# A fused attention and convolution kernel: band weights turned in half pieces, weight maxima over memory, buffers moved, and the end of attention rearranged

## The chip, the cores and the metric

The kernel runs on one core of a Trainium2 chip. The metric is the device time of that core in microseconds: 3374.07 us before, the median of three runs (3363.94 to 3385.05). Five engines work side by side and meet at semaphores: TensorE (PE, with its weight loads as PEld), VectorE (DVE), ScalarE (ACT), GpSimd (POOL) and SyncE (SP, which issues nearly all DMAs).

## The reference, cut to what matters

The input x is (4, 128, 128, 128) in float32. Layer 0 cuts each image into overlapping 16x16 regions with a step of 14, normalises, attends inside each region with four heads, adds x, merges the overlaps, normalises again, projects to 256 channels, runs a depthwise 5x5 convolution, normalises over the batch, applies GELU twice and projects back. Layer 1 is two 3x3 convolutions with quantised activations and weights.

```python
attn = jax.nn.softmax(jnp.einsum('bhqd,bhkd->bhqk', q, k) * hd ** (-0.5), axis=-1)
o = jnp.einsum('bhqk,bhkd->bhqd', attn, v)
tok = o @ w_out + b_out + tok
...
ym = jax.lax.conv_general_dilated(ym, dw_k, window_strides=(1, 1), padding=[(2, 2), (2, 2)], feature_group_count=HIDDEN, ...)
...
alpha = jnp.max(jnp.abs(w)) + 1e-12
wc = jnp.clip(w / alpha, -1.0, 1.0)
q = jnp.round(wc * n) / n * alpha
```

## The kernel before

**Bands and regions.** Attention goes over 36 bands: four images, nine bands each, a band being sixteen rows. A band t has nine regions j. For each region the main loop (L834 to L850) issues `scores(j)`, then `last()`, which is the `values` step of the region before, then three lists of side work, with `halves(j)` and `values_in(j)` between them. The engines PE, ACT, DVE and SP execute in the order written here; only POOL's order is chosen by the scheduler. Every DMA that SP issues stands in one queue, so a DMA that has to wait holds all behind it.

**Side work.** `beside(t)` (L765) makes the nine triples of lists. The steps `a1`, `a2` are the first normalisation and the q and k projections of the next band's two row blocks (`ln1_chunks`); `b1`, `b2` are the output projection, the residual `xf`, the second normalisation and the projection `p0` to 256 channels of the last band's two row blocks (`post_chunks`). In both, a step of squares (ACT), one of sums on TensorE (L345), one of Ln and Exp on ACT that writes a small row of 1/deviation to memory (L362), one that reads it back spread over 128 partitions (`spread`, L367), and one that multiplies by it on DVE (`scaled`, L376). In `b1` and `b2` the multiply is step 6 and the four projections `p0` are steps 7 to 10.

**Conv steps.** The depthwise convolution is done on TensorE with band matrices, in units: one for each of the first three images (33 steps each), and three for the last image (17 steps each), whose rows come free only late. `conv_steps` (L545) gives a step that loads two tiles ahead, then one step a tile: load weights `w` (two DMAs) and rows `u` (four DMAs) for the tile after next, the products (L600), copies to `c` on ACT (L607), statistics on DVE (L611), and stores to `cv_d`. The list `todo` holds all steps that wait for a place; each band takes `share[0]` of them and sets each behind one region's side work: L792 names the order in which regions are filled.

```python
            conv = [todo.pop(0) for _ in range(min(share[0], len(todo)))]
...
            for j in sorted((0, 3, 5, 7, 1, 2, 8, 4, 6)[: len(conv)]):
                c[j] = [conv.pop(0)]
```

The unit over rows 64 to 95 of the last image enters `todo` at band 35 and gets nine places there; its last eight steps run in the tail.

**Preparation in the first bands.** `todo` begins with the quantisation of the two 3x3 weights (`quantised`, L281: load, largest, scales and clip, widen, to_int, to_f8) and with `band_matrices` (L202), which builds the depthwise band matrices over memory: zero edges, padded taps, 32 writes into `band_d`, then twelve pieces that are loaded, turned (outer two of three indices exchanged, L256) and stored to `dw_d`. Three places a band are used, so this takes bands 0 to 7. The turn of a piece is one copy of 40x2048, on ACT where the piece's s is odd and on DVE otherwise; one step turns two pieces and loads the next two. All these tiles share the three buffers of `scratch` (L198).

**Buffers.** `xp` (three) holds x row blocks `xt` that `load_ahead` (L409) loads from within the multiply step of the block in the same place one band earlier; `xfp` (one) holds `xf`, which is read until the multiply `b[6]`.

**The tail.** After the last region, `beside(T)` (L784) gives the `b` steps of the last band, with the eight conv steps that are left set between them, while POOL issues the sixteen loads of all conv weights `all_w` for the last unit (L861). Then the last unit runs with its own tiles: four loads ahead, products into the score tiles `sc`, stores by the ACT queue. After that follow the statistics and the gelu and 3x3 stages, which the change does not touch.

Of the kernel before, what the change touches and what calls it, by code (L numbers as in the profile page):

```python
# [14 lines left out]
P = 128  # L15
# [7 lines left out]
LB = 8  # L23
# [23 lines left out]
def layers(  # L47
# [127 lines left out]
    with ExitStack() as actx:  # L175
# [5 lines left out]
        work, dev, xnp, xfp = pool("work", 1), pool("dev", 2), pool("xnp", 3), pool("xfp", 1)  # L181
# [7 lines left out]
        xp, yp, sums = pool("xp", 3), pool("yp", 2), pool("sums", 1)  # L189
# [8 lines left out]
        def scratch(n):  # L198

            return up.tile([P, 32 * CW], F32, name="u")[:, :n]  # L200

        def band_matrices():  # L202
# [50 lines left out]
            def turn(c, s):  # L253
                by_c = scratch(32 * 64)[:KD]
                copy = nc.scalar.copy if s % 2 else nc.vector.tensor_copy
                copy(by_c.rearrange("p (c m) -> p m c", m=32), held.pop((c, s)))  # L256
                nc.sync.dma_start(
                    out=dw_d[c // 16 : (c + 64) // 16, :, s, :].rearrange("k p n -> p k n"),
                    in_=by_c.rearrange("p (k n) -> p k n", n=16 * 32),
                )  # L260

# [8 lines left out]
            steps = [several(zeros, *each(edges, [(b,) for b in range(B)])), padded_taps]  # L270
            for n in range(0, GR, 2):
                steps.append(several(*each(by_outputs, [(ro,) for ro in range(n, n + 2)])))
            steps += [lambda: None]

            for n in range(0, len(pieces) + 2, 2):
                steps.append(
                    several(*each(turn, pieces[max(n - 2, 0) : n]), *each(load, pieces[n : n + 2]))
                )
            return steps

        def quantised(n, w):  # L281
# [14 lines left out]
            def largest():  # L296
                am = small.tile([P, 1], F32, name="am")
                nc.vector.tensor_reduce(am, held["w"], AX.X, ALU.max, apply_absolute_value=True)
                held["alpha"] = small.tile([P, 1], F32, name="alpha")
                nc.gpsimd.partition_all_reduce(held["alpha"], am, P, bass_isa.ReduceOp.max)  # L300

            def scales():
                alpha = held["alpha"]
                nc.vector.tensor_scalar(alpha, alpha, 1e-12, None, ALU.add)
                nc.vector.tensor_scalar(ks, alpha, 1.0 / 105.0, None, ALU.mult)
                held["ra"] = small.tile([P, 1], F32, name="ra")
                nc.vector.reciprocal(held["ra"], alpha)
# [19 lines left out]
            return [load, largest, clip_all, widen, to_int, to_f8]  # L327
# [153 lines left out]
        def post_chunks(t):  # L481
# [4 lines left out]
            for at, (r, n) in enumerate(finished(t)):  # L486
# [5 lines left out]
                def project(hh, r=r, n=n, at=at, held=held):  # L492
                    if hh == 0:
                        room = tail[0] if tail and at else xfp
                        held["xf"] = room.tile([P, LB * P], F32, name="xf")
# [269 lines left out]
        def beside(t):  # L765
# [5 lines left out]
            if t >= 2:  # L771
                b, i = bands[t - 2]
                if i == NR - 1 and b < B - 1:
                    todo.extend(conv_steps(b))
                    share[0] = -(-len(todo) // (NR if b < B - 2 else 5))
                elif b == B - 1 and i == 4:
                    todo.extend(conv_steps(B - 1))
                    share[0] = NR
                elif b == B - 1 and i == 6:
                    todo.extend(conv_steps(B))  # L780
            conv = [todo.pop(0) for _ in range(min(share[0], len(todo)))]
            a1, a2 = one if one else ([None] * 9,) * 2
            b1, b2 = two if two else ([None] * 11,) * 2
            if t == T:  # L784
                c = conv + [None] * (9 - len(conv))
                return [
                    *b1[:2], *b2[:2], b1[2], b1[3], b2[2], b2[3], b1[4], b2[4], *c[:3], b1[5], b2[5],
                    *c[3:6], b1[6], *b1[7:], b2[6], *b2[7:], *c[6:],
                ]

            c = [[] for _ in range(NR)]
            for j in sorted((0, 3, 5, 7, 1, 2, 8, 4, 6)[: len(conv)]):  # L792
                c[j] = [conv.pop(0)]
            x1 = lambda: fetch(t, 0)
            x2 = lambda: fetch(t, 1)
            return [
# [4 lines left out]
                ([], [b1[6], a2[3], a1[5], a1[6], *c[4]], [b2[0], b2[1], b2[2]]),  # L801
                ([b2[3]], [a1[7], a1[8], *c[5]], [b2[4], a2[4], b1[7], b1[8]]),
                ([], [b2[5], b1[9], b1[10], *c[6]], [a2[5], a2[6]]),
                ([], [b2[6], x1, a2[7], a2[8]], c[7]),
                ([], [x2, b2[7], b2[8], *c[8]], [b2[9], b2[10]]),
            ]

# [8 lines left out]
        todo, share = [], [3]  # L816
        wq, kscale, tail = [], [], []
        for pair in zip(quantised(0, w1), quantised(1, w2)):
            todo.append(lambda pair=pair: [s() for s in pair])
# [9 lines left out]
        with nullcontext() if safe else tc.manual_schedule(engines=MANUAL):  # L829
# [27 lines left out]
            all_w = []  # L857
            for n, s in enumerate(beside(T)):
                if len(all_w) < NCK:
                    all_w.append(tail[0].tile([P, 3, 16, 32], F32, name=f"w{n}"))  # L860
                    weights(all_w[n], n, 0, 2, nc.gpsimd.dma_start)  # L861
                run([s])
            flush(len(stores))
            run(todo)
            for s in conv_steps(len(units) - 1, 4, (all_w, tail[1])):
                s()
                flush(len(stores), nc.scalar)

# [380 lines left out]
```

## Time and profile before

| what | value |
|---|---|
| median of three runs | 3374.07 us |
| profiled execution | 3383.11 us, of which the span is 3381.3 |
| mean granted TensorE clock | 0.960 |
| attention, first scores to last values | 35.4 to 2282.5 us |
| tail and last depthwise unit | 2282.5 to 2424 us |
| gelu and 3x3 stages | 2424 to 3381 us |
| memory traffic | 682.64 MB, 202 GB/s over the span |

The busy shares and the 40 slices say where TensorE is not at work; a window over one band gives its length and the busy time of each engine in it; the timeline then shows which instruction TensorE waited for there, and, from the instruction named, what that one had waited for. A wait for several semaphores is put down to the one that came last. A row of the timeline reads: start, length, engine, line, operation, written and read tiles, shape, count, and in brackets the idle time of the engine before it and what ended it.

The wait totals that the change bears on, over the whole run: POOL `sm` for ACT `pt` 629.7 us (125 times), PE L600 for loads of `u` 33.2 us (13), PE L446 for the DVE multiply 26.8 us (10), PE L345 for the residual `xf` 13.6 us (5), DVE multiply for the spread 60.2 us (22); on SP, waits for the rows of 1/deviation in front of L367, L386 and L569 231.8, 175.4 and 133.7 us.

### The profile page before, as it was taken

To read this page: it belongs to the slowest core of one execution; us is meant where nothing else is said; L and a number is where in the kernel's file an instruction comes from. 1 tells how busy PE (TensorE), PEld (TensorE's weight loads), DVE (VectorE), ACT (ScalarE), POOL (GpSimd) and SP (SyncE) were. 2 spreads that over 40 slices of the span, in tenths; PEclk is the share of its full clock that TensorE was granted. 3 is DMA by queue.
4 is the path that set the end of the run, shared out by engine and by line. 5 is a ranking of instruction groups with operands and counts; after the bars stand their busy time and mean duration, and the time that the engine had idled before them with its cause. 6 is when DMAs were issued, how large, how long until landed. Compare 5 with 4: busy or idle time off the path is not lost. (4 is left out here: it accounts for less than half of the span.)

```text
span 3381.3 us, 75962 instructions
## 1 busy us (share of the span) xinstructions
PE 3144.9 (93%) x30922; PEld 1584.0 (47%) x30922; DVE 2006.5 (59%) x3229; ACT 2006.7 (59%) x2818; POOL 841.9 (25%) x1060
## 2 busy tenths in 40 slices
PE   6999889999999999999999999984799999999998
PEld 3555445555454554554444445552544444444343
DVE  4767666766766666666655555551455555666543
ACT  4677667666666666666655556551267677433433
POOL 2443334333333333333322222220011111000000
PEclk8999989999999999999999999896599999999999
DMA  2455655788887788878699988877699999552298
GB/s 89 131 155 148 157 137 142 185 195 190 190 199 178 184 181 195 195 189 194 157 203 206 203 193 191 206 188 198 175 360 359 359 356 316 166 174 81 77 358 312
DMA packets 812012, 682.64 MB, mean 202 GB/s; under 512 B 581550, under 2 KB 696327, under 8 KB 811655
## 3 DMA queue, kind: packets, MB, share of 16 engines
q1 hardware_dynamic: 792071, 669.03, 72.8%
q10 hardware_dynamic: 18560, 4.72, 0.6%
q8 instruction: 247, 4.05, 0.5%
q0 software_dynamic: 1024, 3.93, 0.4%
q14 instruction: 110, 0.90, 0.1%
HBM read 410.68 MB, written 270.81 MB: 202 GB/s over the span
## 5 line engine op out<-in xcount | busy, mean ns | idle before, releaser
L751 DVE RECIPROCAL rd<-po 128x256 f32<-128x256 f32 x324 | 569.4, 1757 | 513.5 <-PE po L739 511.3
L1023 PE MATMUL pc<-q,wq 128*128 128x512 fp8e4 x3168 | 702.0, 381 | 14.4 <-DVE q L1035 14.4
L676 ACT ACTIVATE pt<-sc 128x1024 f32<-128x1024 f32 x648 | 626.2, 1019 | 96.5 <-PE sc L668 64.2
L686 POOL TENSOR_TENSOR sm<-pt 128x512 f32<-128x512 f32 x324 | 417.7, 1289 | 1064.3 <-ACT pt L676 629.7
L1023 PEld LDWEIGHTS <-wq 128*128 128x128 fp8e4 x3168 | 309.1, 98 | 417.6 <-issue 50.0
L600 PE MATMUL pm<-u,w 40*32 40x504 f32 (+5 forms) x7680 | 370.9, 497 | 48.3 <-DMA u<-y_d 33.2
L668 PE MATMUL sc<-q,kr 32*128 32x256 f32 x5184 | 402.4, 405 | 1.9 <-ACT pt L676 1.7
L731 PE MATMUL po<-pt,v 128*32 128x256 f32 x5184 | 349.9, 388 | 26.8 <-ACT v L660 16.7
L611 DVE BATCH_NORM_STATS2 st<-c 128x6 f32<-128x512 f32 (+2 forms) x384 | 175.4, 506 | 255.5 <-ACT c L607 254.7
L668 PEld LDWEIGHTS sc<-q,kr 32*128 32x128 f32 x5184 | 247.8, 185 | 150.3 <-issue 105.1
L607 ACT COPY c<-pm 128x512 f32<-128x512 f32 (+1 forms) x256 | 132.4, 562 | 288.9 <-PE pm L600 247.3
L446 PE MATMUL pm<-xn,wqkv 128*128 128x512 f32 (+1 forms) x576 | 270.2, 594 | 29.1 <-DVE xn L376 26.8
L515 PE MATMUL pm<-xn,wp 128*128 128x512 f32 (+1 forms) x576 | 259.7, 575 | 8.0 <-DVE xn L376 7.8
L656 PEld LDWEIGHTS pm<-wqkv,yr 128*128 128x128 f32 x1296 | 183.4, 194 | 177.5 <-issue 100.6
L600 PEld LDWEIGHTS pm<-u,w 40*32 40x32 f32 x7680 | 161.3, 110 | 218.4 <-issue 139.6
L1081 PE MATMUL pb<-cv,wp 128*128 128x512 f32 x512 | 232.6, 598 | 12.2 <-ACT cv L1072 12.2
L686 DVE TENSOR_TENSOR sm<-pt 128x512 f32<-128x512 f32 x324 | 228.2, 704 | 11.9 <-ACT pt L676 11.9
L520 ACT ACTIVATE y<-pm,bp 128x512 f32<-128x512 f32 (+1 forms) x288 | 180.5, 640 | 80.2 <-PE pm L515 73.8
L731 PEld LDWEIGHTS po<-pt,v 128*32 128x32 f32 x5184 | 137.1, 109 | 193.8 <-issue 47.8
L656 PE MATMUL pm<-wqkv,yr 128*128 128x128 f32 x1296 | 221.1, 294 | 1.8 <-DVE rstd L352 1.1
L739 PE MATMUL po<-sm,ones 128*32 128x256 f32 x2592 | 201.6, 381 | 8.0 <-POOL sm L686 8.0
L1031 DVE BATCH_NORM_STATS2 st<-pc 128x6 f32<-128x512 f32 x256 | 165.6, 689 | 67.3 <-PE pc L1023 67.3
(149 smaller groups left out, 3468.0 us busy)
## 6 DMA issues: line engine op xcount, KB each, us to landing
cv<-cv_d SPq DMA_DIRECT2D x64, 1024.0 KB
u<-y_d SPq DMA_DIRECT2D x224, 256.0 KB
cv_d<-c SPq DMA_DIRECT2D x192, 256.0 KB
xn<-row SPq DMA_DIRECT2D x80, 512.0 KB
y_d<-y SPq DMA_DIRECT2D x160, 256.0 KB
xfl<-xf_d SPq DMA_DIRECT2D x64, 512.0 KB
id_d<-y SPq DMA_DIRECT2D x64, 512.0 KB
idt<-id_d SPq DMA_DIRECT2D x64, 512.0 KB
```

The lines of the kernel that those rows point to most:

```text
L446: nc.tensor.matmul(pm[:, : n * P], wqkv[:, m * P : (m + 1) * P], held["xn"][hh], start=True, stop=True,)
L515: nc.tensor.matmul(pm[:, : n * P], wp0[:, h, :], held["xn"][hh], start=True, stop=True)
L600: nc.tensor.matmul(pc[half][32 * q : 32 * q + 32, j, :, a:z], wt[hs, s, c0 + c, :], ut[hs, :, c, a + s - 1 : z + s - 1], start=(s == 1), s ...
L656: nc.tensor.matmul(pv[:, c, :], region(yr, j)[:, c * P : (c + 1) * P], wqkv[:, 2 * P :], start=True, stop=True)
L668: nc.tensor.matmul(sc[h // 2][:, h % 2, kc, :].rearrange("p (r c) -> p r c", c=RS), region(kr, j)[hs, kc * P : (kc + 1) * P], queries(j, h ...
L676: nc.scalar.activation(pt, sc[p], AF.Exp)
L686: add(sm, pt[:, :, 0, :], pt[:, :, 1, :], ALU.add)
L731: nc.tensor.matmul(po[hs, 0, :], v[:, kc, hs], pt[h // 2][:, h % 2, kc, :], start=(kc == 0), stop=(kc == 1),)
L739: nc.tensor.matmul(po[hs, 1, :], ones, sm[h // 2][:, h % 2, :], start=True, stop=True)
L751: nc.vector.reciprocal(rd, po[:, 1, :])
L1023: nc.tensor.matmul(pc[:, h], w[:, t, :], q1[b][:, r + dy : r + dy + RB, dx : dx + P], start=(t == 0), stop=(t == 8),)
L1081: nc.tensor.matmul(pb[:, m], wp2[:, h, :], cv[:, h, px], start=(h == 0), stop=(h == 1))
```

## The change

- `xfp` gets two buffers, `xp` goes from three to two.
- `turn` copies half a piece at a time, always on DVE, in two steps; the next piece is loaded with the first half. Zeros, edges and band writes become single steps.
- The maximum over partitions is no longer a GpSimd all-reduce: the 128 partial maxima are written to memory as a row, read back into every partition as a 128x128 tile (`spread`), and reduced on DVE. The two weights' steps go one after the other, shifted by one, instead of in pairs.
- Seven places a band instead of three for this preparation, which then takes bands 0 to 8.
- The side plan is rearranged: `b1[6]` one region later, `b1[7..10]` and `a2[6]` after it.
- In band 35 the share is 18, two conv steps a region (`c[j]` and `d[j]`), so all 17 steps of that unit run there.
- The tail chain holds no conv steps; half of `all_w` is loaded by SP before it, the other half by SP after the first steps of the last unit. The second `xf` of the tail comes from `xfp`.

```diff
-        work, dev, xnp, xfp = pool("work", 1), pool("dev", 2), pool("xnp", 3), pool("xfp", 1)
+        work, dev, xnp, xfp = pool("work", 1), pool("dev", 2), pool("xnp", 3), pool("xfp", 2)
...
-        xp, yp, sums = pool("xp", 3), pool("yp", 2), pool("sums", 1)
+        xp, yp, sums = pool("xp", 2), pool("yp", 2), pool("sums", 1)
...
-            def turn(c, s):
-                by_c = scratch(32 * 64)[:KD]
-                copy = nc.scalar.copy if s % 2 else nc.vector.tensor_copy
-                copy(by_c.rearrange("p (c m) -> p m c", m=32), held.pop((c, s)))
-                nc.sync.dma_start(
...
+            def turn(c, s, half):
+                if half == 0:
+                    held["c"] = scratch(32 * 64)[:KD]
+                by_m, by_c = held[c, s], held["c"]
+                nc.vector.tensor_copy(
+                    by_c[:, half * 1024 : half * 1024 + 1024].rearrange("p (c m) -> p m c", m=32),
+                    by_m[:, :, 32 * half : 32 * half + 32],
+                )
+                if half:
+                    del held[c, s]
+                    nc.sync.dma_start(
...
-            for n in range(0, len(pieces) + 2, 2):
+            for n, p in enumerate(pieces):
                 steps.append(
-                    several(*each(turn, pieces[max(n - 2, 0) : n]), *each(load, pieces[n : n + 2]))
-                )
+                    several(lambda p=p: turn(*p, 0), *each(load, pieces[n + 1 : n + 2]))
+                )
+                steps.append(lambda p=p: turn(*p, 1))
...
-                held["alpha"] = small.tile([P, 1], F32, name="alpha")
-                nc.gpsimd.partition_all_reduce(held["alpha"], am, P, bass_isa.ReduceOp.max)
+                held["row"] = row = rowp.tile([4, 256], F32, name="row")
+                store(row[0:1, :P].rearrange("a p -> p a"), am)
+
+            def spread():
+                row = held["row"]
+                held["am"] = small.tile([P, P], F32, name="ams", bufs=1)
+                nc.sync.dma_start(out=held["am"], in_=bass.AP(row.tensor, row.offset, [[0, P], [1, P]]))
...
+                nc.vector.tensor_reduce(alpha, held["am"], AX.X, ALU.max)
...
                 elif b == B - 1 and i == 6:
                     todo.extend(conv_steps(B))
+                    share[0] = 2 * NR
...
-                    *b1[:2], *b2[:2], b1[2], b1[3], b2[2], b2[3], b1[4], b2[4], *c[:3], b1[5], b2[5],
-                    *c[3:6], b1[6], *b1[7:], b2[6], *b2[7:], *c[6:],
+                    *conv, *b1[:2], *b2[:2], b1[2], b1[3], b2[2], b2[3], b1[4], b2[4], b1[5], b2[5],
+                    b1[6], *b1[7:], b2[6], *b2[7:],
...
-                ([], [b1[6], a2[3], a1[5], a1[6], *c[4]], [b2[0], b2[1], b2[2]]),
-                ([b2[3]], [a1[7], a1[8], *c[5]], [b2[4], a2[4], b1[7], b1[8]]),
-                ([], [b2[5], b1[9], b1[10], *c[6]], [a2[5], a2[6]]),
-                ([], [b2[6], x1, a2[7], a2[8]], c[7]),
+                ([], [a2[3], a1[5], a1[6], *c[4]], [b2[0], b2[1], b2[2]]),
+                ([b2[3]], [b1[6], a1[7], a1[8], *c[5]], [b2[4], a2[4]]),
+                ([], [b2[5], b1[7], b1[8], *c[6]], [b1[9], b1[10], a2[5]]),
+                ([], [b2[6], x1, a2[6], a2[7], a2[8]], c[7]),
                 ([], [x2, b2[7], b2[8], *c[8]], [b2[9], b2[10]]),
             ]
+            return [(one, two, three + d[j]) for j, (one, two, three) in enumerate(plan)]
...
-        todo, share = [], [3]
+        todo, share = [], [7]
...
-            all_w = []
-            for n, s in enumerate(beside(T)):
-                if len(all_w) < NCK:
-                    all_w.append(tail[0].tile([P, 3, 16, 32], F32, name=f"w{n}"))
-                    weights(all_w[n], n, 0, 2, nc.gpsimd.dma_start)
-                run([s])
+            all_w = [tail[0].tile([P, 3, 16, 32], F32, name=f"w{k}") for k in range(NCK)]
+            for k in range(NCK // 2):
+                weights(all_w[k], k, 0, 2, nc.sync.dma_start)
+            run(beside(T))
             flush(len(stores))
             run(todo)
-            for s in conv_steps(len(units) - 1, 4, (all_w, tail[1])):
+            for n, s in enumerate(conv_steps(len(units) - 1, 4, (all_w, tail[1]))):
                 s()
                 flush(len(stores), nc.scalar)
+                if n < NCK // 2:
+                    weights(all_w[NCK // 2 + n], NCK // 2 + n, 0, 2, nc.sync.dma_start)
```

## The prediction

> **What bounds the kernel now.** I read the page first (busy shares, 40 slices), then windows over each band of nine regions (from the first scores matmul, L668, of one band to that of the next), then the timeline wherever TensorE's idle time rose.
>
> ```profile
> PE 3144.9 (93%) x30922; PEld 1584.0 (47%) x30922; DVE 2006.5 (59%) x3229; ACT 2006.7 (59%) x2818; POOL 841.9 (25%) x1060
> ...
> PE   6999889999999999999999999984799999999998
> ...
> PEclk8999989999999999999999999896599999999999
> ```
>
> TensorE is the bound almost everywhere; the dents are in slices 0, 4-5 and around 30.
>
> ```profile
> 297.40:348.70 51.30, 49.41 (x505) 26.88 (x504) 36.06 (x55) 37.12 (x60) 21.65 (x28) 1.00 0.57 149
> 348.70:417.80 69.10, 53.78 (x501) 28.77 (x500) 42.34 (x59) 44.49 (x62) 24.33 (x27) 0.90 0.62 152
> 417.80:485.40 67.60, 54.49 (x502) 29.02 (x502) 42.37 (x59) 44.31 (x61) 23.19 (x24) 0.87 0.57 146
> ...
> 1188.20:1249.00 60.80, 59.70 (x693) 30.50 (x692) 40.80 (x63) 41.16 (x68) 20.98 (x27) 1.00 0.80 190
> 1669.50:1746.20 76.70, 68.82 (x789) 32.73 (x788) 42.97 (x67) 43.95 (x71) 19.48 (x25) 0.96 0.93 188
> ...
> 2216.20:2282.50 66.30, 58.77 (x1245) 35.18 (x1244) 37.88 (x79) 35.32 (x61) 19.09 (x23) 0.95 0.69 177
> 2282.50:2366.00 83.50, 38.95 (x824) 23.54 (x825) 16.45 (x48) 15.65 (x32) 8.33 (x17) 0.64 0.78 198
> 2366.00:2424.00 58.00, 46.06 (x1536) 39.80 (x1536) 25.07 (x125) 10.35 (x32) 0.00 (x0) 0.50 0.63 155
> ```
>
> Columns: stretch, length, busy us of PE, PEld, DVE, ACT, POOL, clock, DMA share, GB/s. A plain band takes 51.3 us; bands 6 and 7, equal in attention work, take 69.1 and 67.6. A band with four conv steps is nearly all matmul (59.7 of 60.8). With seven (bands 28 to 32), TensorE idles 4 to 8 us. From 2282.5, when attention ends, TensorE idles 44.5 of 83.5 us, then works at half clock. After 2424 nothing is changed; the chain of waits is TensorE alone from 2470 on (L1023, L1081), and before that, back to 2254 where it breaks off, it is mostly loads of `u` and stores of `cv_d`: the tail hangs on transfers, the rest on TensorE.
>
> ```profile
> 59.24 0.72 POOL L300 PARTITION_ALL_REDUCE alpha<-am  x2 [5.77 <-issue]
> 60.91 1.07 PE L731 MATMUL po<-pt,v 128*32 128x256 f32 x16
> 69.95 1.08 PE L739 MATMUL po<-sm,ones 128*32 128x256 f32 x8 [7.97 <-POOL sm L686]
> ...
> 354.14 1.95 DVE L256 COPY u<-u 40x2048 f32<-40x2048 f32 x1
> 356.13 3.67 ACT L256 COPY u<-u 40x2048 f32<-40x2048 f32 x1 [3.33 <-DVE u L256]
> 360.07 1.94 PE L731 MATMUL po<-pt,v 128*32 128x256 f32 x16 [7.03 <-ACT v L660]
> ...
> 1710.69 1.29 DVE L376 TENSOR_TENSOR xn<-xn,xf 128x512 f32<-128x512 f32 x2 [5.04 <-DMA xn<-row]
> 1712.76 1.38 PE L345 MATMUL pm<-xf,ones 128*32 128x192 f32 x8 [4.32 <-DVE xf L500]
> ...
> 2307.65 0.48 ACTq L362 DMA_DIRECT2D row<-rstd  x1
> ```
>
> Four causes, one each: the two all-reduces keep POOL from its `sm` (8.0 us); two whole turns, one after the other, keep ACT from `v` (7.0 us, in both bands); the residual's multiply waits for its spread on DVE and the next residual stands behind it (4.3 us); in the tail the first row of rstd, ready at 2298, is issued at 2307.65.
>
> **What the Trainium skill says.** "TensorE: Matmul & The Clock Gate" (What's actually happening) gives half clock after an idle window of about 3.4 us: agreed, 0.64 and 0.50 above, and four L446 matmuls after the all-reduce took 3.78 us where the same four at 57 us took 1.98. "DMA: Bandwidth & Descriptors" (Issuing engines are not separate DMA queues) says that another issuer only saves issue time, so moving weight loads from POOL to SP moves 0.39 us each, no bytes; no run here compares the two. Its section Latency and other measured facts names a fixed cost of about 2 us per DMA, hence an estimate of 4 us for two in a row; here a row written at 16.42 was back, spread over 512 KB, at 21.87: 5.5 us, which I use.
>
> **The change part by part**, against the profiled execution, 3383.1 us (span 3381.3), 9.0 above the median 3374.07.
>
> *Maxima over memory.* POOL loses two all-reduces; added are two 128-element writes, two 64 KB reads on SP and two 128x128 maxima on DVE (about 0.28 us, as L163 of that size). The wait for a trip of 5.5 us or less lies between two conv slots (regions of 5.7 us); what SP holds behind it is x and residual loads wanted a band later. Gone: 8.0 us and about 2 us of cold matmuls. DVE may wait a little for the read, with `rd` behind it. **-9** (-5 to -11).
>
> *Half turns.* Excess of bands 6 and 7: 69.1 + 67.6 - 2 x 51.3 = 34.1 us. In its place 24 half copies, all on DVE, about 1.0 us each (half of 1.95), over bands 5 to 8; the built order shows one a region, behind that region's `sm`. Cover: DVE is busy 36 of 51.3 us in a plain band, so 1.7 us a region is free and `rd` usually waits for PE. I charge 0.2 us each, 5 us: **-29**. Bounds: all 24 exposed, -10; none, -34. Splitting zeros, edges and band writes into single steps moves the same DMAs to other regions of bands whose DMA share is 0.6: nothing, +-2.
>
> *Residual buffer and later multiply.* `b1[6]` moves a region later, so `b2[0]` no longer stands behind a late spread; it needs the second `xf`. In 1669 to 2046 PE waited 12.7 us for `xf`, and a clock of 0.96 over 377 us lost about as much again. Next in line is DMA at 0.93, so I take a third: **-9** (0 to -20). The projections that move (`a2[6]`, `b1[7..10]`) keep their number; where bands are all matmul, 0 (-3 to +6).
>
> *x buffers.* Pool `xp` goes from three to two, so each x load now waits on SP for the DVE multiply of two blocks earlier; behind it stand stores, spreads and conv loads. Comparing, block by block, the end of that multiply with the issue of the load in this trace: in 21 of 70 cases the multiply is later (84 us together, 19 at most), nearly all in bands without conv work; elsewhere it was over by about 4 us. 0, up to +6.
>
> *Last band.* Seventeen steps instead of nine: eight more products at 1.71 us (13.70 us for 8 in this window) are 13.7 us of PE. DMA per step, from the trace's packets: 240 of 1 KB, 160 of 2 KB, 1024 of 256 B at 57, 112 and 19 ns over 16 engines, 3.2 us, eight are 26 on top of 0.69 x 66.3 = 46: 72 us. SP issues some 168 DMAs in the built order at 0.39 us, 66 us. All three come close to each other, so the band becomes about 83 us: **+17** (+13 to +30).
>
> *Tail chain.* From end of attention to the first `sc` matmul of the last unit it is 83.5 us. Without conv, from the rows of before: last values and seams 4.3 (2288.3 less 1.5 of POOL's DMA issues), projection to rstd 9.6, Ln and Exp 0.9, trip 5.5, first multiply 0.7, p0 and y 12.4 (2344.5 to 2356.9; the second spread hides in it), landing 3.5, load 5: 42 us. Four of eight weight pairs now go on SP ahead: 8 issues are 3.1 us, 1.97 MB at about 200 GB/s 10 us, partly in front of the rows: +6. So **-35** (-25 to -41). The last unit stays as it is: half clock, 55 us; the other four weight pairs add 7 us to DMA at 0.63 of 58.
>
> Sum: -9 - 29 - 9 + 17 - 35 = **-65**: 3318 by the profiled execution, **3309** by the median.
>
> **Rivals.**
> - *The end gives it back*: band 35 becomes bound by SP and DMA (+30) and the rows wait behind the weights (-25): +5 in place of -18. For: 168 issues and DMA at 72 us in one band. Against: bands of 88 us run at DMA 0.88 with little idle. 3332.
> - *DVE becomes the bound in bands 5 to 8*: each half turn exposed, and waits for its load: -10 there, 3328.
> - *The x loads hold SP*: slower. A multiply not yet done blocks SP and so the conv loads behind it. At 72 loads, 0.9 us of PE each eats the whole gain; at 1.5 us, 108 - 65 = +43, 3417. It decides only if SP arrives before the multiply in conv bands; the trace has it 4 us late, and PE waited for `u` 33 us in the whole run.
> - *It does not do what it says*: the words say more buffers of x, the diff gives fewer; the half turns could have been put together. The built order shows them apart, so I give it nothing of its own.
>
> **How the numbers follow.** Forecast 0.62 (own range 3280 to 3335), end gives back 0.20, DVE 0.11, x loads 0.07. The first three reach, with their bounds, from 3280 to 3358; outside are the x loads and about a tenth of the rest. About 1%, 34 us, is what a measurement of this kernel can tell from no change: faster if below 3340. Nearly all of the forecast, six in ten of the second and seven in ten of the third fall there: 0.60 + 0.12 + 0.08, less a little: 0.79. Slower is the x loads, 0.07; within 1% 0.14.
>
> **What would show it.** Right: no idle of 7 us on PE up to 500 us; bands 5 to 8 of 51 to 54 us; no `xf` wait over 2 us in bands 28 to 32; band 35 of 80 to 86 us; 45 to 50 us from the end of attention to the first `sc`. Wrong: bands 10 to 27 over 61.5 us, SP waiting for DVE at the x loads there; band 35 over 95 us; rows still issued late behind weights.

## The result, and the profile after

The changed kernel takes 3343.9 us (median of seven runs, 3342.32 to 3353.07) where the kernel before, run beside it, takes 3380.13 (3363.94 to 3385.05). The ratio is 0.9908, 95% interval 0.9887 to 0.9929: faster, by 36 us in the medians and 31 by the ratio, where 65 were forecast. The profiled executions, 3348.1 and 3383.11 us, differ by 35.

In the changed kernel lines stand 10 to 12 lower in attention: scores L679, values L742 and L750, multiply L388, spread L379, row L374, stores L398, turn L257, `w` and `u` loads L551 and L580, conv products L611, copy `c` L618. The page of the profile after, the same rows as before (busy time, then tenths in 40 slices):

```profile
PE 3129.4 (94%) x30922; PEld 1594.7 (48%) x30922; DVE 2008.2 (60%) x3247; ACT 1998.7 (60%) x2814; POOL 815.9 (24%) x1042
...
PE   7996999999999999999999989875699999999998
...
PEclk9998999999999999999999998976599999999999
```

PEclk is full in slice 0 now, but slice 3, which was full, has a dent, and the dents around slice 30 begin earlier. Windows of the profile after, band by band and then the end (columns as before: stretch, length, busy PE, PEld, DVE, ACT, POOL, clock, DMA share, GB/s):

```profile
226.70:294.00 67.30, 51.70 (x501) 28.46 (x500) 35.00 (x55) 37.61 (x60) 20.50 (x28) 0.87 0.43 125
294.00:360.30 66.30, 50.46 (x505) 27.69 (x504) 37.16 (x58) 37.60 (x60) 21.93 (x28) 0.90 0.45 121
360.30:411.20 50.90, 48.53 (x501) 27.07 (x500) 41.68 (x63) 37.38 (x60) 22.27 (x27) 1.00 0.64 171
...
1215.40:1275.20 59.80, 59.23 (x693) 30.69 (x692) 40.59 (x63) 41.50 (x68) 20.26 (x27) 1.00 0.83 199
...
2166.10:2282.70 116.60, 87.92 (x2013) 56.20 (x2012) 45.34 (x111) 41.18 (x77) 17.19 (x20) 0.77 0.65 169
2282.70:2319.30 36.60, 16.78 (x64) 6.79 (x62) 9.34 (x16) 10.00 (x16) 1.78 (x4) 0.79 0.68 192
2319.30:2388.10 68.80, 49.34 (x1536) 39.81 (x1536) 23.42 (x116) 9.70 (x30) 0.00 (x0) 0.50 0.60 156
```

The first two are bands 4 and 5: 67 and 66 us of plain attention that took 51.3 before, at the lowest DMA share of all. The third is band 6; bands 6 and 7, 69.1 and 67.6 before, take 51. The fourth has four conv steps. The last three are band 35, the tail and the last conv unit. All stages of the two profiles, with what the prediction said of each:

| stage | before | after | difference | forecast |
|---|---|---|---|---|
| band 0 | 52.5 | 40.2 | -12.3 | -9 |
| bands 1 to 3 | 158.2 | 152.0 | -6.2 | 0 |
| bands 4 and 5 | 102.6 | 133.6 | +31.0 | 0, but for its part of the 5 us charged for half turns |
| bands 6 to 8 | 188.4 | 154.4 | -34.0 | -29 with band 5 |
| bands 10 to 27 | 1080.6 | 1063.4 | -17.2 | 0 |
| bands 28 to 32 | 376.2 | 360.9 | -15.3 | -9 |
| bands 33 and 34 | 170.6 | 175.4 | +4.8 | 0 |
| band 35 | 66.3 | 116.6 | +50.3 | +17 |
| end of attention to first `sc` | 83.5 | 36.5 | -47.0 | -35 |
| last conv unit | 55.1 | 68.8 | +13.7 | 0 |

What follows takes 960.2 and 958.1 us, the start 1.0 less; band 9 is alike. Bands 4 and 5, band 35 and the last unit lost 95 us that the sum had at 17; the stages that gained brought 132 us that it had at 82. That the total missed by no more than 30 us is luck: errors of 78 and 50 us went opposite ways.

### The profile page after: what moved, and what is told of

The parts are those of the page before. It is cut to its first block, busy times and chain, and to the rows that moved or that the text cites. A ratio compares the mean times of both kernels' runs of the same rounds, so it can differ in the third digit from the quotient of the medians.

```text
span 3346.2 us, 76089 instructions
## 1 busy us (share of the span) xinstructions
PE 3129.4 (94%) x30922; PEld 1594.7 (48%) x30922; DVE 2008.2 (60%) x3247; ACT 1998.7 (60%) x2814; POOL 815.9 (24%) x1042
## 4 chain that ended last, share of the span: by engine, by line
PE 73%; DMA 9%; ACT 7%; DVE 5%; SPq 2%; issue 2%; ACTq 1%; POOL 0%; DVEq 0%; POOLq 0%
PE pc L1040 19%; PE pm L611 9%; PE sc L679 7%; PE pm L458 7%; PE po L742 7%; PE pb L1098 6%; PE pm L526 6%; PE pm L667 4%; PE pm L510 3%; PE po L750 3%; DMA u<-y_d 3%; DMA xn<-row 2%; ACT pt L687 2%; PE pm L357 2%; DMA cv_d<-c 2%
## 5 line engine op out<-in xcount | busy, mean ns | idle before, releaser
L611 PE MATMUL pm<-u,w 40*32 40x504 f32 (+5 forms) x7680 | 378.3, 500 | 42.0 <-DMA u<-y_d 33.7
L679 PE MATMUL sc<-q,kr 32*128 32x256 f32 x5184 | 407.3, 409 | 1.9 <-ACT pt L687 1.7
L742 PE MATMUL po<-pt,v 128*32 128x256 f32 x5184 | 352.2, 390 | 11.7 <-DVE part L766 11.6
L679 PEld LDWEIGHTS sc<-q,kr 32*128 32x128 f32 x5184 | 250.5, 187 | 129.6 <-issue 80.2
L458 PE MATMUL pm<-xn,wqkv 128*128 128x512 f32 (+1 forms) x576 | 262.9, 581 | 50.7 <-DVE xn L388 50.7
L618 ACT COPY c<-pm 128x512 f32<-128x512 f32 (+1 forms) x256 | 132.8, 562 | 295.2 <-PE pm L611 263.8
L611 PEld LDWEIGHTS pm<-u,w 40*32 40x32 f32 x7680 | 167.0, 111 | 208.6 <-issue 119.4
L742 PEld LDWEIGHTS po<-pt,v 128*32 128x32 f32 x5184 | 137.8, 110 | 180.0 <-issue 50.4
L750 PE MATMUL po<-sm,ones 128*32 128x256 f32 x2592 | 201.8, 382 | 0.0
```

The lines of the kernel that those rows point to most:

```text
L458: nc.tensor.matmul(pm[:, : n * P], wqkv[:, m * P : (m + 1) * P], held["xn"][hh], start=True, stop=True,)
L611: nc.tensor.matmul(pc[half][32 * q : 32 * q + 32, j, :, a:z], wt[hs, s, c0 + c, :], ut[hs, :, c, a + s - 1 : z + s - 1], start=(s == 1), s ...
L679: nc.tensor.matmul(sc[h // 2][:, h % 2, kc, :].rearrange("p (r c) -> p r c", c=RS), region(kr, j)[hs, kc * P : (kc + 1) * P], queries(j, h ...
L742: nc.tensor.matmul(po[hs, 0, :], v[:, kc, hs], pt[h // 2][:, h % 2, kc, :], start=(kc == 0), stop=(kc == 1),)
L750: nc.tensor.matmul(po[hs, 1, :], ones, sm[h // 2][:, h % 2, :], start=True, stop=True)
```

## The stall in bands 4 and 5

From the timeline of the profile after, in band 4 (start, length, engine, line, what is written and read, count, in brackets the idle time before and what ended it):

```profile
238.03 0.50 ACTq L374 DMA_DIRECT2D row<-rstd  x1
239.69 5.86 SPq L398 DMA_DIRECT2D y_d<-y  x3
243.54 0.48 ACTq L374 DMA_DIRECT2D row<-rstd  x1
...
248.56 0.48 ACTq L374 DMA_DIRECT2D row<-rstd  x1
...
250.16 2.82 SPq L237 DMA_DIRECT2D band_d<-pad_d  x4
253.09 0.40 SPq L398 DMA_DIRECT2D xf_d<-xf  x1
253.59 0.37 SPq L379 DMA_DIRECT2D xn<-row  x1
...
262.87 1.29 DVE L388 TENSOR_TENSOR xn<-xn,xt 128x512 f32<-128x512 f32 x2 [14.62 <-DMA xn<-row]
...
263.61 3.78 PE L458 MATMUL pm<-xn,wqkv 128*128 128x512 f32 x4 [14.25 <-DVE xn L388]
```

Read it upwards. TensorE waits 14.25 us for the multiply, the multiply for the spread. The row that this spread reads was issued by ACT at 238.03; SP issues the spread only at 253.59. In between SP stores `y_d` and writes `band_d`, and each time starts 1.6 us after another row of ACT: 239.69 after 238.03, 250.16 after 248.56 (the third `y_d` store, at 245.19, after 243.54). None of them reads a row. The DMAs of SP and ACT signal their end on eight semaphores, numbered 101 to 107 and 109 in the trace, which the two engines take in turn: these are the completion counters in the texts below. A DMA waits here until the one before it on its counter has ended. The row of 238.03 and the first `y_d` store share counter 107, the row of 243.54 and the third store 101, the row of 248.56 and the first `band_d` write 102. So SP waits for the third row before it may issue the spread of the first.

That explains the late issue. From its issue to the multiply the spread took 9.3 us more, against 3.8 for the first spread of the kernel before (18.10 to 21.87), while the four writes issued just before it were still in transfer. How much of the 9.3 us is theirs is not shown.

**Pairs again.** First theory: the single writes stand in front of the spread.

```diff
-            steps += each(by_outputs, [(ro,) for ro in range(GR)])
+            for n in (0, 4):
+                steps += [two(n), idle, idle, two(n + 1), two(n + 2), two(n + 3), idle]
```

> The changed kernel, with the writes to band_d in pairs again, in regions 0, 3, 5 and 7 of bands 3 and 4; nothing else differs. Theory (single writes in regions 0 to 2 stand on SP, and on the DMA rings, in front of the spread xn of ln1, which then reaches DVE late): the stalls of 14.3 and 14.5 us at L458 in bands 4 and 5 go, both bands take 51 to 54 us in place of 67.3 and 66.3, and the whole takes 24 to 30 us less than the changed kernel, about 3316. Rival (two buffers of x, not the writes, hold the first multiply): both bands stay at 66 to 67 us and the time at 3344.

Ratio 0.9906 (0.9887 to 0.9925), where the changed kernel has 0.9908. Bands 4 and 5 took 65.7 and 60.5 us, TensorE's waits there 13.8 and 7.5 us, again for the multiply. That theory fell, and its rival, x buffers, was not shown either.

**Writes by POOL.**

```diff
-                    nc.sync.dma_start(
+                    nc.gpsimd.dma_start(
                         out=band_d[2 * ro + eo]
```

> The changed kernel, with the 32 writes to band_d issued by POOL in place of SP, in the same places. Theory (on SP they stand in front of the ln1 spread, and they wait there for rows of rstd that ACT writes only later; the bytes themselves do no harm): SP no longer waits for a row before the spread, the spread is issued within 2 us of its row, bands 4 and 5 take 51 to 54 us each in place of 67.3 and 66.3, the whole 24 to 31 us less than the changed kernel, about 3316. Rival (the writes fill the DMA rings and the spread lands late behind them, whoever issues it): the spread goes out early but DVE still waits 8 us or more for it, bands 4 and 5 stay above 60 us each, the whole is at most 10 us less.

Ratio 0.9839 (0.9822 to 0.9856). Bands 4 and 5: 53.8 and 53.1 us. The bytes are the same and TensorE waits for no multiply in the two bands, so the bytes alone are not the cause. But this edit takes the writes out of SP's order and off the counters together.

**Rows by POOL.** The writes stay on SP, in front of the spread; only the rows leave ACT.

```diff
-                nc.scalar.dma_start(out=row[:, :w], in_=rstd[0:P:32, :])
+                by = nc.gpsimd if 3 <= now[0] <= 5 else nc.scalar
+                by.dma_start(out=row[:, :w], in_=rstd[0:P:32, :])
```

> The changed kernel, with the rows of rstd of bands 3 to 5 issued by POOL in place of ACT; the writes to band_d stay on SP, in their places. Theory (SP's stores and writes wait there for a row that ACT issues later, because the DMAs of SP and ACT take the same few completion counters in turn; the order on SP is harmless otherwise): without ACT's rows on these counters SP reaches the spread of ln1 when its row has landed, and bands 4 and 5 take 51 to 57 us each in place of 67.3 and 66.3, the whole 18 to 30 us less than the changed kernel. Rival (it is the order on SP: the spread stands behind four writes, whatever they wait for): bands 4 and 5 stay at 62 to 68 us each, the whole within 8 us of the changed kernel.

Ratio 0.9827 (0.9810 to 0.9845), bands 4 and 5 49.1 us each, below a plain band of either kernel. The same place in this kernel's timeline:

```profile
226.95 3.29 SPq L399 DMA_DIRECT2D y_d<-y  x3
230.29 4.28 SPq L237 DMA_DIRECT2D band_d<-pad_d  x4
238.20 0.34 SPq L399 DMA_DIRECT2D xf_d<-xf  x1
238.25 0.62 POOL L375 DMA_DIRECT2D row<-rstd  x1 [2.95 <-ACT rstd L372]
242.40 0.34 SPq L380 DMA_DIRECT2D xn<-row  x1
...
247.21 1.28 DVE L389 TENSOR_TENSOR xn<-xn,xt 128x512 f32<-128x512 f32 x2
```

Stores and writes are out before the first row exists, the spread follows its row by 4 us, and DVE has no idle time in front of the multiply. With the same order on SP the stall is gone, so the wait for rows was the cause. The 35.4 us of the two bands are far more than ACT saves by not issuing their eight rows, 0.48 us each.

## Band 35

Two conv steps in the timeline of SP, profile after, and below them what SP's DMAs of the band cost to issue (count; ns minimum, median, maximum; first and last start), asked by line:

```profile
2204.95 1.56 SPq L551 DMA_DIRECT2D w<-dw_d  x2
2206.56 1.57 SPq L580 DMA_DIRECT2D u<-y_d  x4
2208.23 1.94 SPq L398 DMA_DIRECT2D cv_d<-c  x4
2210.27 1.57 SPq L551 DMA_DIRECT2D w<-dw_d  x2
2211.88 1.57 SPq L580 DMA_DIRECT2D u<-y_d  x4
```

```profile
L551 SPq DMA_DIRECT2D w<-dw_d x32: 747/760/789, 2172.4 to 2269.5; - x32
```

```profile
L580 SPq DMA_DIRECT2D u<-y_d x64: 296/324/1536, 2174.1 to 2271.6; - x64
```

```profile
L398 SPq DMA_DIRECT2D cv_d<-c x68: 360/467/1489, 2167.9 to 2281.6; - x68
```

One step is 5.1 us of SP without a gap; two a region make 10.2 us, where a plain region takes 5.7. Weights, `u` and conv stores are 24.4, 26.3 and 35.0 us in all, and SP's issuing in the band, 181 DMAs, is 94. That is what the Trainium skill, in "Perfetto Trace Analysis" (What "DMA-bound" means), lists as its second case: the issuing engine's track is solid with DMA slices, which are time spent making descriptors, not moving data. The trace agrees in part: DMA share 0.65, SP at 94 of 116.6 us.

**Nine steps again**, the tail's order with it:

```diff
-                    share[0] = 2 * NR
...
+                    *b1[:2], *b2[:2], b1[2], b1[3], b2[2], b2[3], b1[4], b2[4], *c[:3], b1[5], b2[5],
+                    *c[3:6], b1[6], *b1[7:], b2[6], *b2[7:], *c[6:],
```

> The changed kernel, with nine conv steps in the last band again, and the other eight between the steps of the tail chain as before. Theory (the last band lost 50 us, more than the tail gained): band 35 takes 66 to 70 us in place of about 116, the stretch from end of attention to the end of the last conv unit about 138 in place of 106, and the whole 14 to 20 us less than the changed kernel: about 3327. Rival (most of the 50 us in band 35 is something else than the eight added steps, such as loads that come late after the change of buffers): band 35 stays above 90 us and the whole is 10 us or more above the changed kernel.

Band 35: 63.4 us, so the 50 us are the eight steps. But from there to the last conv product it took 153.7 us, not 138, since the last unit stayed at 68.7; ratio 0.9906 (0.9886 to 0.9926), the same as with the change.

**Weights by POOL:** `nc.gpsimd.dma_start` for the `w` loads of this unit.

> The changed kernel, with the two weight loads of each conv step of the last band issued by POOL in place of SP. Theory (SP's issuing bounds band 35: 5.1 us a step, two steps a region): SP loses 1.57 us a step, so a region falls from 10.2 to about 7.1 us and then to the next bound, TensorE and DMA at 71 to 75 us a band: band 35 takes 78 to 92 us in place of about 116, the whole 24 to 38 us less than the changed kernel, about 3313. Rival (three buffers of weights and u, two steps ahead, are too few, or the DMA rings themselves are): the issue moves and the landing does not, band 35 stays at 108 to 118 us and the whole at 3338 to 3346.

Band 35: 104.0 us, 12.6 less for 24 us less of weights to issue; between theory and rival. Ratio 0.9893 (0.9873 to 0.9912). In five kernels that are alike in this band it took 111.9 to 118.0 us, so single profiles of it differ by some 6 us.

**Conv stores by ACT as well.**

> The kernel that has POOL issue the weight loads of the last band, with the conv stores of that band issued by ACT as well, so that SP is left with 35 us of issuing of the 94 us that it has in the changed kernel. Theory (what is left of band 35 is still SP's issuing): up to the end of attention it takes 82 to 92 us in place of 104 with POOL's weights and 116.6 in the changed kernel, the whole 10 to 20 us less than with POOL's weights alone. Rival (with 75 us of issuing in 104 SP had ceased to be the bound; loads two steps ahead in three buffers, and TensorE at a lowered clock, are): 98 to 108 us, and the whole within 6 us of the one with POOL's weights.

Band 35: 96.4 us, between the two; ratio 0.9887 (0.9868 to 0.9906). SP's waits in that band say why the rest did not follow:

```profile
SPq L580 <- DMA cv_d<-c: 24.1, 9, 5.5
```

The loads of `u` now waited 24.1 us, nine times, for stores that ACT issues: the counters again.

**Conv stores by POOL**, weights on SP.

> The changed kernel, with the conv stores of the last band issued by POOL in place of SP (weights stay on SP). With ACT as their issuer SP's u loads waited 24.1 us for these stores. Theory (band 35 is SP's issuing, 94 us, and what remained with ACT as issuer was SP waiting for ACT's DMAs through the shared counters): SP is left with 60 us, u loads no longer wait for stores, band 35 takes 84 to 93 us up to the end of attention in place of 116.6, and of 96.4 with weights by POOL and stores by ACT. Rival (loads only two steps ahead, or TensorE at a lowered clock, bound it at 95 to 105 whoever issues): 95 or more.

100.2 us, ratio 0.9855 (0.9829 to 0.9882). Waits of `u` for stores are gone, yet TensorE still waited 15.4 us for `u`, 7.3 of it for the first load, which is issued in the region of its product; and SP's weight loads still waited 8.3 us for rows. So 12 to 20 us of the 50 went with SP's issuing, give or take that spread. A floor of 95 to 105 us (the kernels below among them) remains. Loads only two steps ahead and a clock of 0.84 to 0.87 are candidates; a deeper lookahead was not tried, so that floor stays open.

## The last unit

TensorE's waits there, from the first `sc` matmul on, in the profile after (in all, times, longest), then in the kernel below:

```profile
PE sc L611 <- DMA u<-y_d: 19.8, 11, 6.9
PE sc L611 <- DMA w<-dw_d: 3.7, 1, 3.7
```

```profile
PE sc L611 <- DMA u<-y_d: 7.4, 2, 7.1
PE sc L611 <- issue: 4.0, 6, 0.9
```

**All weights in the tail**, by POOL, as before:

```diff
-            for k in range(NCK // 2):
-                weights(all_w[k], k, 0, 2, nc.sync.dma_start)
-            run(beside(T))
+            for n, s in enumerate(beside(T)):
+                if len(all_w) < NCK:
+                    all_w.append(tail[0].tile([P, 3, 16, 32], F32, name=f"w{n}"))
+                    weights(all_w[n], n, 0, 2, nc.gpsimd.dma_start)
+                run([s])
```

> The changed kernel, with all eight weight pairs of the last conv unit loaded by POOL between the steps of the tail chain, as before, and none within the unit. Theory (the 13.7 us by which the last unit got longer come from four weight pairs that SP issues between its u loads): from the first sc matmul to the last 55 to 58 us in place of 68.8; from the end of attention to the first sc 36 to 44 us in place of 36.5, as more bytes go in front; the whole 7 to 14 us less than the changed kernel, about 3333. Rival (the unit is slower because its u loads are not as far ahead as they were behind other conv work): it stays at 66 to 70 us, the whole at 3343 to 3352.

The unit took 55.0 us, the stretch before it 42.9: 13.8 gained, 6.4 given back. Ratio 0.9891 (0.9875 to 0.9907), an interval too wide to show these 7 us.

SP's own waits in the last unit of the changed kernel, most of them in its first steps, say how the weights did it:

```profile
SPq L580 <- DMA cv_d<-c: 17.0, 8, 7.6
SPq L551 <- DMA cv_d<-c: 5.0, 3, 3.9
```

SP waited 22.0 us for conv stores that ACT issues here and that neither load reads: the counters again. Issuing the eight weight loads took 2.3 us in all. Without weights in the unit there is no such wait: a step then has four `u` loads and four stores, and the eight counters keep apart, 101 and 104 to 106 for the loads, 102, 103, 107 and 109 for the stores. Each pair of weights shifts the turn by two, and loads fall on the counters of stores.

## The order of the steps

**Order and residual buffer as before** (one `xf`, the tail's second from its own pool), then the **order alone**, with two `xf`:

```diff
-                ([], [a2[3], a1[5], a1[6], *c[4]], [b2[0], b2[1], b2[2]]),
-                ([b2[3]], [b1[6], a1[7], a1[8], *c[5]], [b2[4], a2[4]]),
...
+                ([], [b1[6], a2[3], a1[5], a1[6], *c[4]], [b2[0], b2[1], b2[2]]),
+                ([b2[3]], [a1[7], a1[8], *c[5]], [b2[4], a2[4], b1[7], b1[8]]),
```

> The changed kernel, with the order of the steps in a band and the one buffer of the residual as before (the multiply b1[6] back in region 4, a2[6] and the b1 projections a region earlier). Theory (this part freed bands 28 to 32 of 15 us, and also made the bands with four conv steps 1.1 us shorter each): bands 28 to 32 take 372 to 378 us in all in place of 361, bands 10 to 26 about 60.9 each in place of 59.8, the whole 26 to 36 us more than the changed kernel, about 3374. Rival (the 1.1 us of each conv band come from the two buffers of x or from chance): only bands 28 to 32 lose, 9 to 16 us, and the whole is about 3355.

> The changed kernel, with the order of the steps in a band as before, and the second buffer of the residual kept. Theory (the order alone, with the first multiply of the second norm and the projections a region later, made each band with four conv steps 1.1 us shorter): bands 10 to 27 take 1078 to 1082 us in all as before, in place of 1063.4, the whole 20 to 36 us more than the changed kernel, as with order and buffer both undone (3386 us, 1080.4). Rival (the second residual buffer did it): bands 10 to 27 stay at 1062 to 1066 us, the whole at 3343 to 3355.

Ratios 1.0010 (1.0000 to 1.0021) and 0.9993 (0.9984 to 1.0003); bands 10 to 27 took 1080.4 and 1079.5 us, bands 28 to 32 371.2 and 370.1, bands 1 to 3 157.5 and 156.1, bands 6 to 8 157.8 and 157.3. So the order alone took some 16 us out of the bands that the prediction held for all matmul: idle time per conv band fell from 1.1 to 0.6 us, and PE's busy time by half a microsecond. Over the whole run, undoing the order alone costs 0.0085 of the time before, about 29 us, nearly all that the change gains. TensorE's waits in bands 10 to 27, before and after, are almost all for ACT's squares:

```profile
PE pm L345 <- ACT sq L339: 16.1, 34, 0.7
```

```profile
PE pm L357 <- ACT sq L351: 10.6, 19, 0.7
```

Why PE's busy time fell too is not shown. Bands 10 to 27 of the second kernel have two x buffers and the length of the kernel before, which has three: x loads cost nothing there. Of bands 28 to 32 nothing so exact can be said: in eleven kernels that are alike there they took 360.9 (the changed kernel itself) to 375.9 us, mean 368.2, and the two with the order as before lie within that range.

## The repairs together

**Three repairs** (writes, all weights of the last unit and band 35's weights by POOL, its conv stores by ACT), and **nine steps with the first two**:

> The changed kernel with three repairs together: the writes to band_d by POOL, all weights of the last unit by POOL within the tail chain, and in the last band the weights by POOL and the conv stores by ACT. Theory (the three places don't touch each other): 27 + 8 + 20 us less than the changed kernel, about 3290; bands 4 and 5 of 51 to 54 us, band 35 of 92 to 100, the last unit of 55 to 58. Rival (what one repair gains, the next stage waits for, as in bands 28 to 34, whose length differs by 10 us between kernels that are alike there): 3305 or more.

> The kernel that has nine conv steps in the last band and eight in the tail chain, with the writes to band_d by POOL and all weights of the last unit by POOL within the tail. Theory (two steps a region pay once SP is relieved of a part of its issuing): band 35 takes 63 to 66 us, end of attention to last conv product 136 to 144, together 199 to 210 where the kernel with all three repairs has 190 to 200: 5 to 15 us more than that kernel. Rival (two steps a region gain nothing even then): the two are within 4 us.

Ratios 0.9803 (0.9777 to 0.9828) and 0.9812 (0.9791 to 0.9833). The three repairs gained 36 us on the changed kernel, of 55 expected; band 35 took 104.6 us, where the same two edits had given 96.4. Band 35 up to the last conv product: 205.5 and 203.8 us. Two steps a region were worth nothing here.

**All rows by POOL**, in every band, first in the kernel with nine steps and all weights in the tail, then with two steps a region and conv stores by POOL:

> The changed kernel with all rows of rstd, in every band, by POOL; nine conv steps in the last band and eight in the tail; all weights of the last unit by POOL within the tail. Theory (waits for rows through shared counters also cost the bands of six to eight conv steps, where SP's u and w loads wait 38 us for rows): bands 28 to 34 take 505 to 530 us in place of 536, bands 3 to 5 49.1 each, the whole 38 to 60 us less than the changed kernel: about 3295. Rival (there it is transfers and TensorE's clock; and rows by POOL come later, since POOL issues them between its own work): bands 28 to 34 at 535 to 560 us, the whole 3305 to 3325.

> The same with two conv steps a region in the last band, whose conv stores POOL issues. Theory (SP then has 60 us of issuing in band 35): band 35 84 to 93 us, end of attention to last conv product 94 to 102, together 180 to 195 where nine steps and eight in the tail took 203.8: 9 to 24 us less than the kernel with nine. Rival (what the band loses the tail gains, as with the first three repairs, 205.5): within 4 us of it.

Ratios 0.9596 (0.9571 to 0.9622) and 0.9579 (0.9552 to 0.9606); medians 3255.01 and 3248.28 us, the best of all. Windows of the second: band 4, a conv band, band 35.

```profile
223.40:272.50 49.10, 48.34 (x502) 27.07 (x501) 34.89 (x55) 37.40 (x59) 22.27 (x32) 1.00 0.58 168
1161.70:1220.50 58.80, 58.80 (x693) 30.70 (x692) 40.02 (x63) 41.47 (x68) 22.61 (x31) 1.00 0.88 198
2087.70:2182.80 95.10, 77.75 (x2013) 50.05 (x2012) 45.37 (x111) 41.21 (x77) 64.69 (x86) 0.87 0.75 206
```

The conv band has no idle time on TensorE at all. Bands 28 to 34 took 521.0 and 519.3 us against 536.3 in the changed kernel and up to 549.6 in those alike. The two ends, 203.2 and 193.4 us, differ by 10, the kernels by less than their intervals.

**Rows by POOL in the kernel before, and in the changed kernel, nothing else:**

> The kernel before, with all rows of rstd by POOL in place of ACT, and nothing else. Theory (the kernel before had such waits too, but none that TensorE felt in bands 0 to 9, and a few us in each of bands 28 to 34): bands 2 to 5 stay at 51 us each, bands 28 to 34 take 520 to 540 us in place of 546.8, the whole 5 to 25 us less than the kernel before. Rival (the waits of SP were never late enough there): within 4 us of the kernel before, or slower where POOL issues the rows late.

> The changed kernel, with all rows of rstd by POOL in place of ACT, and nothing else: the pair to the kernel before with the same edit (3324 us). Theory (without the waits through shared counters the change is worth its parts: band 0 -12, bands 6 to 8 -38, the order -13 in bands 10 to 27, and at the end +50 in band 35, -47 up to the first sc, +14 in the last unit: -46): 3268 to 3290 us, 34 to 56 less than the kernel before with rows by POOL; bands 4 and 5 of 49.1 us each. Rival (the change gains no more than its measured 1% there either): 3290 to 3315.

3324.16 us, ratio 0.9815 (0.9786 to 0.9844), and 3270.09 us, ratio 0.9659 (0.9641 to 0.9677). So rows by ACT cost the kernel before some 63 us too, 23 of them in bands 10 to 27 (1057.8), spread thin; and with rows by POOL in both, the change is worth 54 us, not 36 (53 and 31 by the ratios).

This edit does two things, and no run parts them: SP no longer waits for rows, and ACT no longer issues them, 144 times 0.48 us or some 70 us in all. In bands 10 to 27 only the second is seen in TensorE's waits. From the timeline of the changed kernel:

```profile
1234.17 0.48 ACTq L374 DMA_DIRECT2D row<-rstd  x1
1234.70 0.84 ACT L351 ACTIVATE sq<-xt 128x768 f32<-128x768 f32 x1 [0.56 <-ACT rstd L372]
...
1235.60 0.53 PE L357 MATMUL pm<-sq,ones 128*32 128x192 f32 x8 [0.56 <-ACT sq L351]
```

ACT's squares stand behind the row, and TensorE waits for them for as long as the row took to issue. With rows by POOL these waits fall from 16.1 to 2.8 us in the kernel before and from 10.6 to none in the changed one, and in none of the four is a wait of TensorE for a DMA listed in these bands. The rest of the 23 us is a shorter busy time of PE, which is not explained. So of the 63 us a part, not known exactly, is ACT's issuing and not waits through counters. The counters themselves are seen in SP's waits for rows over the whole run, in the changed kernel and the same with rows by POOL, whose DMAs signal on eight semaphores of their own (111 to 118):

```profile
SPq L398 <- DMA row<-rstd: 212.5, 35, 12.7
SPq L379 <- DMA row<-rstd: 160.6, 51, 6.7
SPq L580 <- DMA row<-rstd: 102.6, 28, 6.4
...
SPq L237 <- DMA row<-rstd: 24.3, 4, 8.4
...
SPq L551 <- DMA row<-rstd: 18.5, 6, 4.9
```

```profile
SPq L379 <- DMA row<-rstd: 345.7, 115, 7.4
```

Only the spread (L379) reads the row. In the second kernel it alone waits for it.

## Why the prediction was right and wrong

- **Splitting the writes, "nothing, +-2": +31.** This step failed most. It looked at the DMA share, 0.6, and the bytes; with the same bytes, issued by POOL, the stall was gone. What decided was which DMA of ACT each DMA of SP waits for. The sign was in the totals for the kernel before: its stores (L386) waited 175.4 us for rows that they don't read. The prediction priced such moves as if only data made a DMA wait.
- **Last band, "168 DMAs at 0.39 us, 66 us" of SP: 181 of them, 94 us.** The price was mis-sized: weights cost 0.76, conv stores 0.47, `u` 0.32 us in the middle, 0.52 on average. The trace of before had it: in its band 35 SP issues 97 DMAs in 51.8 us, 0.53 each. The band took +50 instead of +17, 12 to 20 of it from SP's issuing. The edits of the issuers brought it to 95 to 105 us, not to 83: a sum of the busiest engine leaves out that a load issued in the region of its product makes TensorE wait, 7.3 us in one case. The rest of that gap stays open.
- **"The last unit stays as it is": +13.7.** The sum charged the weights that SP issues between its `u` loads only as bytes. They shifted the counters, and SP waited 22.0 us for ACT's stores.
- **Tail chain, -35: -47.0.** Right in kind, 12 us more. The terms of the chain came out near or below their prices: 4.5, 9.7, 5.3, 0.7, 10.5, 3.0 and 2.8 us, where loads had been put at 5 and p0 and y at 12.4. The 6 us charged for weights in front were not paid: SP had issued all eight loads by 2288.84, and the first row went out at 2296.91.
- **Moved projections, "0 (-3 to +6)": -17.2.** A band of 60.8 us with 59.7 us of PE was taken for full. The order alone closed half of its idle time, most of which was TensorE waiting for ACT's squares, and shortened PE's own time. With rows by POOL in both kernels 13 us of it remain (1057.8 against 1044.5).
- **Maxima over memory, -9: -12.3** in band 0, and **half turns, -29: -34.0** in bands 6 to 8, of which 3 are the order's. Right in place and size, though no run undoes either alone; the 8.0 us wait for POOL is gone from band 0, and three bands of half turns take 154.4 us, where three plain ones took 154. The 5 us charged for half turns did not show there.
- **Residual buffer and later multiply, -9:** -15.3 in the profiled pair, -8.0 to the mean of eleven kernels. The mechanism came: TensorE's waits for `xf` in bands 28 to 34, 12.7 us before, are gone. But waits for the multiply and for `u`, 7.4 and 6.5 us, became 10.4 and 10.9, and the kernel with order and buffer as before took 371.2 us, within the range of the eleven. So what it is worth is not shown.
- **x buffers, 0:** right, by the kernel with the order as before. SP did wait for the multiply at x loads, 98.7 us over the run in 24 cases (84 us in 21 were counted), and TensorE did not feel it in bands 10 to 27.
- **Half clock, "agreed, 0.64 and 0.50".** For the last unit that reading does not hold. With all weights in the tail, TensorE was never idle for more than 0.95 us from 2341.93 on, and the clock stayed at 0.50 to the end of the unit at 2396. So it was not idle windows that kept it there; what did is open.

Of the rivals, *the end gives it back* was nearest: its SP bound came (+50, not +30), but rows did not wait behind weights, and the end gave +17.0 in place of -18. *DVE* and *x loads* fell. Of the signs of being right, only "no `xf` wait over 2 us in bands 28 to 32" came out; "no idle of 7 us on PE up to 500 us" failed at 264 and 331 us, band 5 took 66.3 us, band 35 116.6, and the way to the first `sc` was 36.5, shorter than its 45 to 50. Of the signs of being wrong, "band 35 over 95 us" came.

## What to carry to other kernels

When a wait of a DMA names a transfer that it has no data from, look for what they share: order and counters couple queues that nothing in the code couples, and moving a DMA by a region can turn a harmless wait into a stall elsewhere. Ask also what else stands on the issuing engine: a DMA issued on ACT delays the ACT work behind it. Price DMA issues by form, from the rows of the same queue, and ask for each moved load how long before its use it is issued. A band that is 98% matmul can still give 2%.

## What the hardware showed that was not expected

- Moving 144 rows (one for each row block of each norm) from ACT to POOL, the bytes unchanged, took 2.5% off the changed kernel (ratio 0.9908 to 0.9659). The Trainium skill, in "DMA: Bandwidth & Descriptors" (Issuing engines are not separate DMA queues), says that another issuer only saves the time to initiate a DMA; that may cover much of the gain outside bands 4 and 5, since ACT spent some 70 us on issuing all rows. In bands 4 and 5 the measurement goes beyond it: 35.4 us for eight rows of 0.48, because in this program the issuer also decides which DMAs wait for each other.
- A DMA's issue on SP took, in the middle, 0.32 us for `u`, 0.47 for conv stores, 0.68 for memory-to-memory writes, and 0.76 for weights over 40 partitions.
- The DMAs that waited for a row began 1.6 us after ACT began to issue it.
- The clock stayed at 0.50 through the last unit with all weights in the tail, in which TensorE was busy 47 of 55 us, with no gap of a microsecond after the first product.
